# A graph layer on one core: the result is brought to token order by VectorE in 32x32 blocks, with channels laid out to match

## Chip, cores, metric

The kernel runs on one core of a Trainium2 chip. The metric is the device time of one execution in microseconds, as the median of several runs. The first runs of the kernel before gave 1919.82 us (1917.07 to 1921.12, three runs). All ratios below are taken between runs on the same chip in the same call.

## The reference

Input x has 32 batches of 512 tokens with 256 channels; adj has 32 matrices of 512x512, symmetric, with zeros and ones. All is float32. Cut to what matters (`_bn`, `_conv1d` and the set-up of weights are left out):

```python
h0 = relu(layernorm(x))                                   # h below; "x" of the inner layer
xc = transpose(h0)                                        # channels x tokens
h = relu(_bn(_conv1d(xc, conv1_w, 0)))                    # 1 tap
h = _bn(_conv1d(h, conv2_w, 8))                           # 17 taps
x_conv = transpose(relu(h + xc))
s = h0 @ w_se.T + b_se                                    # 3 features
A = exp(-dist(s, s)) * adj
msg = relu(h0 @ w_msg.T + b_msg)
x_nmp = einsum('bnm,bmd->bnd', A, msg)
gi = concat([x_conv, x_nmp]) @ w_ih.T + b_ih              # 768 columns: r, z, n
gh = h0 @ w_hh.T + b_hh
r, z = sigmoid(gi_r + gh_r), sigmoid(gi_z + gh_z)
n = tanh(gi_n + r * gh_n)
return x + (1 - z) * n + z * h0
```

## The kernel before

The program has five stages. The 32 batches come in two halves of 16. Each half has a *conv stage* (normalise, transpose to channels, conv1, a Fourier transform along the tokens; in the first half also that of the weights) and then a *node loop* (messages, A, aggregation, with the Fourier products between them). At the end a *gate stage* works through 16 pairs of batches with the gate products, the blend, and the result. The conv and gate stages are emitted in a fixed order; the node loops are ordered by a scheduler. Inside the gate stage everything lies as channels x tokens, so the result has to be turned to tokens x channels before x can be added and the sum stored.

The parts that the change touches (cuts marked with `# ...`):

```python
work  = ... tc.tile_pool(name="work",  bufs=2)      # lasts over both halves
early = ... tc.tile_pool(name="early", bufs=1)
# pools "first" (conv stage) and "nodes" (node loop) open and close in turn, in the same room

def load_x(b, queue=nc.sync):
    X[b] = pools["work"].tile([P, NC, D], FP, tag="x", name=f"x_{b}", bufs=3)
    queue.dma_start(X[b], x[b].rearrange("(p c) d -> p c d", c=NC))

def normalise(b):
    mv, rstd = STATS.pop(b)
    XN[b] = X[b]                                    # in place
    # ...

def transpose_h(b):
    # ... hT and hs: two tiles of channels x tokens from one PSUM bank
    for dc in range(DC):
        # ... four TensorE transposes into p
        nc.vector.tensor_scalar(HT[b][:, dc, :], p, 0.0, None, op0=ALU.max)
        nc.scalar.activation(HS[b][:, dc, :]..., p.rearrange("p (c q) -> p q c", c=NC), AF.Relu)
    nc.sync.dma_start(HD[b], HT[b])

def message(b):                                     # node loop
    # ...
    nc.tensor.matmul(p[:, : D + NS], HT[b][:, ic, c * P : (c + 1) * P], wmsg[:, ic, :], ...)

def affinity(b):                                    # node loop
    # ...
    nc.vector.transpose(at..., ADJ[b].rearrange("p j (q c) -> p c j q", c=NC)[:, mc])
    nc.vector.tensor_mul(..., by_chunk(at))         # both read with a step of four floats

def finish(p, j, chunks=((0, 1), (2, 3)), wait_for=None):   # gate stage
    xb = XP[p][j]
    # ...
    for bk, i, c, dc in sorted(todo, ...):          # 8 per batch, 256 in all
        nc.tensor.transpose(bk[:, i, dc * P : (dc + 1) * P], NT[p][:, dc, j, c * P : (c + 1) * P], ident)
    for bk, cs in zip(banks, chunks):
        nc.vector.tensor_add(xo, xo, bk[:, : len(cs)])
        nc.sync.dma_start(out[b]..., xo)

def first_part(g, xf, between):                     # conv stage of half g
    for b in range(b0, b0 + 3):
        if b not in X:
            load_x(b)
    statistics(b0)
    normalise(b0)
    statistics(b0 + 1)
    if g == 0:
        transpose_h(b0)
    normalise(b0 + 1)
    if g > 0:
        transpose_h(b0)
    # ...
```

Of the kernel before, what the change touches and what calls it, by code (L numbers as in the profile page):

```python
# [57 lines left out]
def gnn_layer(  # L58
# [40 lines left out]
    X, ADJ, XN, HT, HS, H1, MSG, A, NMP, ST, SL, SR = ({} for _ in range(12))  # L99
    XP, HP, NP, CP, YT, RZ, NT = ({} for _ in range(7))  # L100

    def load_x(b, queue=nc.sync):
        X[b] = pools["work"].tile([P, NC, D], FP, tag="x", name=f"x_{b}", bufs=3)
        queue.dma_start(X[b], x[b].rearrange("(p c) d -> p c d", c=NC))


    load_x(0)
# [10 lines left out]
    nc.scalar.dma_start(w1, w1T.rearrange("(c p) o -> p c o", p=P))  # L118
# [7 lines left out]
    at, n = {}, 0  # L126
    for name in VEC:
        w = GC if name in ("b_ih", "b_hh") else DC
        at[name] = vec[:, n : n + w]
        n += w  # L130
    brz = consts.tile([P, 2 * DC], FP, name="brz")
    nc.vector.tensor_add(brz, at["b_ih"][:, : 2 * DC], at["b_hh"][:, : 2 * DC])
    b_in, b_hn = at["b_ih"][:, 2 * DC :], at["b_hh"][:, 2 * DC :]

    def batch_norm(k):
        scale = consts.tile([P, DC], FP, name=f"{k}_scale")
        shift = consts.tile([P, DC], FP, name=f"{k}_shift")
        nc.vector.tensor_scalar(scale, at[k + "_v"], BN_EPS, None, op0=ALU.add)
        nc.gpsimd.tensor_tensor(scale, scale, minus_half[:, :DC], op=ALU.pow)
        nc.vector.tensor_mul(scale, scale, at[k + "_g"])  # L140
        nc.vector.tensor_mul(shift, at[k + "_m"], scale)
        nc.vector.tensor_sub(shift, at[k + "_b"], shift)
        return scale, shift

    scale1, shift1 = batch_norm("bn1")
    scale2, shift2 = batch_norm("bn2")

# [12 lines left out]
    for c in range(DC):  # L160
# [8 lines left out]
        partial(nc.sync.dma_start, wmsg[:, :, :D], w_msgT.rearrange("(c p) o -> p c o", p=P)),  # L169
        partial(nc.sync.dma_start, wmsg[:, :, D:], w_seT.rearrange("(c p) t -> p c t", p=P)),  # L170
        partial(nc.sync.dma_start, bmsg[:, :D], b_msg.to_broadcast([P, D])),
        partial(nc.sync.dma_start, bmsg[:, D:], b_se.rearrange("t o -> o t").to_broadcast([P, NS])),
    ]
# [55 lines left out]

    def statistics(b):  # L230
# [11 lines left out]
    def normalise(b):  # L242
        mv, rstd = STATS.pop(b)
        XN[b] = X[b]
        for c in range(NC):
            nc.vector.tensor_scalar(
                XN[b][:, c, :], X[b][:, c, :], mv[:, c, 0:1], rstd[:, c : c + 1],
# [4 lines left out]


    def by_chunk(t):

        return t.rearrange("p (q c) -> p c q", c=NC)

    def transpose_h(b):
        HT[b] = work.tile([P, DC, N], FP, tag="hT", name=f"hT_{b}")
        HS[b] = pools["first"].tile([P, DC, N], FP, tag="hs", name=f"hs_{b}", bufs=2)  # L260
        for dc in range(DC):
            p = bank(f"phT_{b}_{dc}")
            for c in range(NC):
                nc.tensor.transpose(p[:, c * P : (c + 1) * P], XN[b][:, c, dc * P : (dc + 1) * P], ident)  # L264
            nc.vector.tensor_scalar(HT[b][:, dc, :], p, 0.0, None, op0=ALU.max)
            nc.scalar.activation(HS[b][:, dc, :].rearrange("p (q c) -> p q c", c=NC),  # L266
                                 p.rearrange("p (c q) -> p q c", c=NC), AF.Relu)
        nc.sync.dma_start(HD[b], HT[b])
        if b % GB != GB - 1:
            del HT[b]  # L270
        del XN[b]

    def conv1(b):
        H1[b] = pools["first"].tile([P, NC, D], FP, tag="h1", name=f"h1_{b}", bufs=2)
        h = N // D
        for c0 in range(0, NC, h):
            p = bank(f"pc1_{b}_{c0}").rearrange("p (c d) -> p c d", d=D)
            for j in range(h):
                c = c0 + j
                for ic in range(DC):  # L280
                    nc.tensor.matmul(p[:, j, :], HS[b][:, ic, c * P : (c + 1) * P], w1[:, ic, :],  # L281
# [4 lines left out]
        del HS[b]  # L286
# [26 lines left out]
    def product(pw, g, u, xf):  # L313
# [21 lines left out]
        nc.scalar.copy(y[:, 0:2, :], p.rearrange("p (k d) -> p k d", d=D))  # L335
        if u == 0:
            nc.vector.memset(y[:, 2, :], 0.0)
        else:
            nc.vector.tensor_copy(y[:, 2, :], p2[:, :D])
# [12 lines left out]

    def message(b):
        MSG[b] = pools["nodes"].tile([P, NC, D], FP, tag="msg", name=f"msg_{b}", bufs=3)
        ST[b] = pools["nodes"].tile([P, 2, NC, NS], FP, tag="st", name=f"st_{b}", bufs=2)
        h = N // D
        for c0 in range(0, NC, h):
            m = MSG[b][:, c0 : c0 + h, :]
            for j in range(h):
                c = c0 + j  # L360
                p = bank(f"pm_{b}_{c}")
                for ic in range(DC):
                    nc.tensor.matmul(p[:, : D + NS], HT[b][:, ic, c * P : (c + 1) * P], wmsg[:, ic, :],  # L363
# [16 lines left out]
    def factors(b):  # L380
# [9 lines left out]
        nc.scalar.copy(t, p)  # L390

    def affinity(b):
# [7 lines left out]
        for mc in range(NC):  # L400
# [3 lines left out]
            nc.vector.transpose(at.rearrange("p (j k) -> p j k", k=32), ADJ[b].rearrange("p j (q c) -> p c j q", c=NC)[:, mc])  # L404
            nc.vector.tensor_mul(*(t.rearrange("p (c q) -> p c q", c=NC) for t in (A[b][:, mc, :], e)), by_chunk(at))  # L405
# [26 lines left out]
    def combine_weights():  # L432

        steps = []
        for k, src in enumerate((w_hhT, w_ihT[D:], w_ihT[:D])):
            w, t = (pools["sums"].tile([P, n, 3, P], FP, tag=f"w{n}", name=f"w{n}_{k}") for n in (4, 7))
            a = src.rearrange("(c p) (g i o) -> p c i g o", p=P, i=2, o=P)
            for j in range(4):
                nc.sync.dma_start(w[:, j], a[:, j // 2, j % 2])
            a11, a21, a12, a22 = (w[:, j] for j in range(4))  # L440
            for dst, x1, x2, op in ((Q5, a21, a22, ALU.add), (Q6, t[:, Q5], a11, ALU.subtract),
                                    (Q7, a11, a21, ALU.subtract), (Q3, a12, t[:, Q6], ALU.subtract)):
                steps.append(partial(nc.gpsimd.tensor_tensor, t[:, dst], x1, x2, op=op))
            stores = [(Q1, a11), (Q2, a12), (Q4, a22)] + [(q, t[:, q]) for q in (Q5, Q6, Q7, Q3)]
            steps[-1] = partial(self_and_store, steps[-1], k, stores)
        return steps

    def self_and_store(step, k, stores):
        step()
        for q, src in stores:  # L450
            nc.sync.dma_start(WS[k][:, q], src)
# [22 lines left out]
    def load_pair_x(p):  # L474
        XP[p] = []
        for b in (2 * p, 2 * p + 1):
            load_x(b)
            XP[p].append(X.pop(b))
# [12 lines left out]
    def inverse(p):  # L491

        CP[p] = pools["ops"].tile([P, 7, N], FP, tag="cp", name=f"cp_{p}")
        for j in range(2):
            for oc in range(DC):
# [7 lines left out]
                xq, hq = (t.rearrange("p (c q) -> p c q", c=NC) for t in (xc, HP[p][:, 2 * oc + j, :]))  # L503
# [355 lines left out]
```

## Time and profile before

| | kernel before |
|---|---|
| median of the first three runs | 1919.82 us |
| span of the profiled run | 1919.7 us, clock 0.991 |
| TensorE busy | 1880.5 us, 98% |
| VectorE, ScalarE, GpSimd busy | 61%, 29%, 29% |
| the result's TensorE transposes | 256 |

The span is the time from the first to the last instruction of the profiled run. The clock is the TensorE clock that was granted, as a share of full speed. An engine is busy while it has an instruction in work, and it is off the path where no other engine waits for it. To evacuate is to copy a result out of the PSUM bank that TensorE wrote it to.

The profile is read from the engine that has no slack. TensorE is that engine here, so the useful question for every instruction is whether TensorE performs it or waits for it. The prediction shows the page, the stages and the groups that carry this; they aren't repeated. One view of the kernel before is added because the argument later turns on it. It is the timeline of the loads of x for the second half and of that half's first transposes (columns: start in us, duration, engine, line, operation, output<-inputs, count).

```profile
135.15 1.10 SPq L104 DMA_DIRECT2D x<-in_x_dram  x1
...
478.98 1.04 PE L264 MATMUL phT<-ident,x 128*128 128x128 f32 x8
481.11 3.78 PE L281 MATMUL pc<-w,hs 128*128 128x256 f32 x16 [1.09 <-ACT hs L266]
```

The second half's first x was asked for before the *first* half's conv stage had ended, more than 300 us ahead of its use; the next load followed at 145 us, and both batches were normalised by 159 us. No bracket with a wait follows the line at 478.98: TensorE goes from the last Fourier product of the node loop straight on to the transposes of the second half.

### The profile page before, as it was taken

Reading aid. Unit: us, or ns where it says so; the run is one execution under the profiler, and the core shown is the slowest. Engines: PE = TensorE matmul, PEld = TensorE weight load, DVE = VectorE, ACT = ScalarE, POOL = GpSimd, SP = SyncE. Lnnn points to the kernel's source line nnn. Section 1 sums busy time; section 2 is a strip of 40 time slices with the busy share of each in tenths; the row PEclk is TensorE's granted clock in tenths of the full one; section 3 lists DMA queues with packets and bytes.
Section 4 is the critical chain, followed back from the end, with each engine's and each line's share of the span. In section 5 each row is a group of like instructions: output and inputs, shape, how many; then the busy total and the mean of one; then the engine's idle time right before and its main releaser. Section 6 shows DMA issues by size and latency. Waiting matters only on the chain.

```text
span 1919.7 us, 21244 instructions
## 1 busy us (share of the span) xinstructions
PE 1880.5 (98%) x7232; PEld 1142.9 (60%) x7232; DVE 1166.6 (61%) x2197; ACT 556.8 (29%) x994; POOL 562.7 (29%) x554
## 2 busy tenths in 40 slices
PE   7999999999999999999999999999999999999998
PEld 5776666666887666765545555555545554555453
DVE  6876777675886667676255535553555445544565
ACT  3665323332444232232212222122212221222121
POOL 3231443433332344445321232213221322133210
PEclk8999999999999999999999999999999999999999
DMA  7998888875668887878342144304440344124400
GB/s 202 297 283 242 248 234 241 258 205 174 204 208 213 236 268 226 254 223 275 93 129 74 55 129 129 100 37 122 129 124 29 106 129 129 37 92 129 129 31 36
DMA packets 220474, 309.87 MB, mean 161 GB/s; under 512 B 14807, under 2 KB 158711, under 8 KB 220367
## 3 DMA queue, kind: packets, MB, share of 16 engines
q1 hardware_dynamic: 200895, 250.93, 44.6%
q0 software_dynamic: 7248, 25.73, 5.0%
q10 hardware_dynamic: 12224, 31.86, 4.6%
q8 instruction: 58, 0.95, 0.2%
q14 instruction: 49, 0.40, 0.1%
HBM read 201.57 MB, written 106.89 MB: 161 GB/s over the span
## 4 chain that ended last, share of the span: by engine, by line
PE 94%; DVE 3%; DMA 2%; issue 0%; ACT 0%; SPq 0%; POOL 0%; DVEq 0%; ACTq 0%; POOLq 0%
PE pg L511 29%; PE pn L511 15%; PE pn L413 11%; PE py L334 11%; PE pc L500 6%; PE pc L281 6%; PE pm L363 5%; PE px L295 3%; PE pw L214 2%; PE pd L399 2%; PE phT L264 1%; PE po L635 1%; PE psr L388 1%; DMA wd<-wst 1%; DMA wt<-wd 0%
## 5 line engine op out<-in xcount | busy, mean ns | idle before, releaser
L511 PE MATMUL pg<-hp,sw 128*128 128x512 f32 x448 | 229.7, 595 | 1.7 <-DVE u L543 1.7
L511 PE MATMUL pg<-np,sw 128*128 128x512 f32 x448 | 229.8, 595 | 0.0
L511 PE MATMUL pg<-cp,sw 128*128 128x512 f32 x448 | 229.1, 593 | 0.0
L413 PE MATMUL pn<-A,msg 128*128 128x512 f32 x512 | 225.0, 593 | 0.0
L489 POOL TENSOR_TENSOR hp<-hp 128x512 f32<-128x512 f32 x64 | 83.1, 1309 | 464.1 <-DMA hp<-hd 331.4
L413 PEld LDWEIGHTS pn<-A,msg 128*128 128x128 f32 x512 | 97.3, 190 | 110.4 <-issue 107.7
L327 POOL TENSOR_TENSOR both<-xf 128x256 f32<-128x256 f32 x78 | 72.8, 934 | 302.4 <-PE py L334 277.4
L405 DVE TENSOR_TENSOR A<-e,at 128x512 f32<-128x512 f32 x128 | 149.0, 1205 | 18.3 <-ACT e L402 18.2
L526 ACT ACTIVATE rz<-rz,brz 128x512 f32<-128x512 f32 x96 | 69.3, 721 | 301.6 <-DVE rz L530 301.6
L334 PE MATMUL py<-wt,both 128*128 128x256 f32 x624 | 151.9, 387 | 3.5 <-DMA adj<-in_adj_dram 3.5
L511 PEld LDWEIGHTS pg<-cp,sw 128*128 128x128 f32 x448 | 85.6, 191 | 107.5 <-issue 107.5
L511 PEld LDWEIGHTS pg<-np,sw 128*128 128x128 f32 x448 | 85.6, 191 | 107.4 <-issue 107.4
L489 POOL TENSOR_TENSOR cp<-cp 128x512 f32<-128x512 f32 x64 | 80.3, 1265 | 221.2 <-ACT cp L505 220.0
L334 PEld LDWEIGHTS py<-wt,both 128*128 128x128 f32 x624 | 115.5, 192 | 47.6 <-issue 31.4
L511 PEld LDWEIGHTS pg<-hp,sw 128*128 128x128 f32 x448 | 82.8, 190 | 94.1 <-issue 88.9
L404 DVE STREAM_TRANSPOSE at<-adj 128x512 f32<-128x512 f32 x128 | 134.6, 1091 | 0.0
L281 PE MATMUL pc<-w,hs 128*128 128x256 f32 x512 | 123.3, 397 | 3.0 <-ACT hs L266 3.0
L500 PEld LDWEIGHTS pc<-back,yt 120*128 120x128 f32 x1024 | 116.9, 192 | 7.6 <-issue 7.6
L311 POOL TENSOR_TENSOR wsum<-wt 128x512 f32<-128x512 f32 x78 | 101.7, 1303 | 67.0 <-DMA wt<-wd 60.0
L363 PE MATMUL pm<-wmsg,hT 128*128 128x259 f32 x512 | 118.1, 383 | 0.0
L500 PE MATMUL pc<-back,yt 120*128 120x80 f32 (+1 forms) x1024 | 116.2, 274 | 0.0
L511 PE MATMUL pn<-hp,sw 128*128 128x512 f32 x224 | 115.2, 596 | 0.0
(113 smaller groups left out, 2821.7 us busy)
## 6 DMA issues: line engine op xcount, KB each, us to landing
wt<-wd SPq DMA_DIRECT2D x160, 256.0 KB, 4.9
adj<-in_adj_dram SPq DMA_DIRECT2D x128, 256.0 KB, 5.6
yd<-y ACTq DMA_DIRECT2D x80, 384.0 KB, 5.1
yt<-yd SPq DMA_DIRECT2D x60, 480.0 KB, 9.8
wd<-wst SPq DMA_DIRECT2D x64, 320.0 KB, 5.2
x<-in_x_dram SPq DMA_DIRECT2D x38, 512.0 KB, 5.6
hd<-hT SPq DMA_DIRECT2D x32, 512.0 KB, 4.3
nd<-nmp SPq DMA_DIRECT2D x32, 512.0 KB, 3.9
```

The costliest lines, as they stand in the source:

```text
L281: nc.tensor.matmul(p[:, j, :], HS[b][:, ic, c * P : (c + 1) * P], w1[:, ic, :], start=(ic == 0), stop=(ic == DC - 1))
L311: nc.gpsimd.tensor_tensor(t, WT[g, u][:, 0], WT[g, u][:, 1], op=ALU.add)
L327: nc.gpsimd.tensor_tensor(both[:, 0], re, im, op=ALU.add)
L334: nc.tensor.matmul(dst, v[:, ic, :], w[:, ic, :], start=(ic == 0), stop=(ic == DC - 1))
L363: nc.tensor.matmul(p[:, : D + NS], HT[b][:, ic, c * P : (c + 1) * P], wmsg[:, ic, :], start=(ic == 0), stop=(ic == DC - 1))
L404: nc.vector.transpose(at.rearrange("p (j k) -> p j k", k=32), ADJ[b].rearrange("p j (q c) -> p c j q", c=NC)[:, mc])
L405: nc.vector.tensor_mul(*(t.rearrange("p (c q) -> p c q", c=NC) for t in (A[b][:, mc, :], e)), by_chunk(at))
L413: nc.tensor.matmul(p, MSG[b][:, mc, dc * P : (dc + 1) * P], A[b][:, mc, :], start=(mc == 0), stop=(mc == NC - 1))
L489: nc.gpsimd.tensor_tensor(t[:, dst, :], t[:, a, :], t[:, b, :], op=sub)
L500: nc.tensor.matmul(bk[:, t0:t1], YT[p][j * W + w][:, oc * P : (oc + 1) * P], back[:, u0 : u0 + t1 - t0], start=(w == 0), stop=(w == W - 1) ...
L511: nc.tensor.matmul(bk, sw[:, k, q, o, :], terms[k][q], start=(first and i == 0), stop=(i == len(ks) - 1), skip_group_check=True)
L526: nc.scalar.activation(rz[:, g, j, :], src, AF.Sigmoid, bias=brz[:, g : g + 1], scale=1.0)
```

## The change

The intent is to take the 256 transposes of the result off TensorE. The VectorE transposes of both kernels work within 32x32 blocks (the prediction names the page on this). So the channels are put in a new order, in which 32-channel pieces of each quarter alternate between the two halves, and x, the weights and the vectors are loaded to match. A block transpose of the result by VectorE then lies as the output wants it. With the tokens in plain order, adj needs no step of four floats in the node loop; instead ScalarE makes the chunks of the message matmuls by copying h (`hq`). The second copy of the transposed h (`hs`) goes. The core of the diff (loads of the vectors and weights, the combination of the gate weights, and the last pair's code are cut):

```diff
     def load_x(b, queue=nc.sync):
-        X[b] = pools["work"].tile([P, NC, D], FP, tag="x", name=f"x_{b}", bufs=3)
-        queue.dma_start(X[b], x[b].rearrange("(p c) d -> p c d", c=NC))
+        X[b] = pools["first"].tile([P, NC, D], FP, tag="x", name=f"x_{b}", bufs=3)
+        queue.dma_start(X[b], x[b].rearrange("(c p) d -> p c d", p=P))
 ...
     def normalise(b):
         mv, rstd = STATS.pop(b)
-        XN[b] = X[b]
+        XN[b] = pools["first"].tile([P, NC, D], FP, tag="xn", name=f"xn_{b}", bufs=2)
 ...
     def transpose_h(b):
-        HS[b] = pools["first"].tile([P, DC, N], FP, tag="hs", name=f"hs_{b}", bufs=2)
 ...
-            nc.scalar.activation(HS[b][:, dc, :].rearrange("p (q c) -> p q c", c=NC),
-                                 p.rearrange("p (c q) -> p q c", c=NC), AF.Relu)
 ...
     def message(b):
+        hq = pools["nodes"].tile([P, DC, N], FP, tag="hq", name=f"hq_{b}", bufs=2)
+        for ic in range(DC):
+            nc.scalar.copy(chunks(hq[:, ic, :]), by_chunk(HT[b][:, ic, :]))
 ...
-                    nc.tensor.matmul(p[:, : D + NS], HT[b][:, ic, c * P : (c + 1) * P], wmsg[:, ic, :],
+                    nc.tensor.matmul(p[:, : D + NS], hq[:, ic, c * P : (c + 1) * P], wmsg[:, ic, :],
 ...
-            nc.vector.transpose(at.rearrange(...), ADJ[b].rearrange("p j (q c) -> p c j q", c=NC)[:, mc])
-            nc.vector.tensor_mul(*(t.rearrange("p (c q) -> p c q", c=NC) for t in (A[b][:, mc, :], e)), by_chunk(at))
+            nc.vector.transpose(at.rearrange(...), ADJ[b][:, :, 32 * mc : 32 * (mc + 1)])
+            nc.vector.tensor_mul(A[b][:, mc, :], e, at)
 ...
+    def to_tokens(p, j, dc):
+        if (p, j) not in OUT:
+            OUT[p, j] = pools["late"].tile([P, N // 32, D // 4], FP, tag="o", name=f"o_{p}_{j}", bufs=2)
+        nc.vector.transpose(OUT[p, j][:, :, 32 * dc : 32 * (dc + 1)], NT[p][:, dc, j, :].rearrange("p (j k) -> p j k", k=32))
+
+    def finish(p, j):
+        last = p == B // 2 - 1
+        for dc in range(0 if last else DC):
+            to_tokens(p, j, dc)
         xb = XP[p][j]
-        (eight TensorE transposes, two sums from PSUM, two stores)
+        nc.vector.tensor_add(xb, xb, OUT.pop((p, j)))
+        for g in range(4):
+            queue = nc.scalar if last and g % 2 else nc.sync
+            queue.dma_start(quarter(out[2 * p + j], g), xb[32 * g : 32 * (g + 1)])
```

The line in parentheses stands for the loops shown under the kernel before, and `(...)` for unchanged text.

## The prediction

> **What bounds the kernel now.** I read the page first: its busy totals, its slices and its chain of waits.
>
> ```profile
> span 1919.7 us, 21244 instructions
> PE 1880.5 (98%) x7232; PEld 1142.9 (60%) x7232; DVE 1166.6 (61%) x2197; ACT 556.8 (29%) x994; POOL 562.7 (29%) x554
> ...
> PE   7999999999999999999999999999999999999998
> ...
> PE 94%; DVE 3%; DMA 2%; issue 0%; ACT 0%; SPq 0%; POOL 0%; DVEq 0%; ACTq 0%; POOLq 0%
> ```
>
> TensorE is busy from the second slice to the last but one, and 94% of the chain that ended last is TensorE. No other engine passes 61%. So time on VectorE or ScalarE counts only where TensorE waits for it, and a TensorE instruction removed counts in full. To see where TensorE waits I asked for sums over five stretches, which are the kernel's stages: conv and DFT of the first half, its node loop, conv and DFT of the second half, its node loop, and the gate stage (columns: stretch, its length, then busy time and instructions of each engine, clock, DMA share, GB/s).
>
> ```profile
> 0.00:174.00 174.00, 159.15 (x901) 115.00 (x902) 128.79 (x367) 98.59 (x207) 48.19 (x75) 0.97 0.90 260
> 174.00:451.00 277.00, 273.13 (x1101) 184.12 (x1100) 200.46 (x393) 84.33 (x160) 105.44 (x107) 0.99 0.81 233
> 451.00:596.00 145.00, 137.99 (x740) 117.47 (x739) 102.37 (x262) 64.48 (x138) 46.46 (x52) 0.98 0.62 204
> 596.00:901.00 305.00, 299.86 (x1202) 201.15 (x1201) 212.44 (x406) 89.97 (x170) 130.20 (x135) 0.99 0.83 238
> 901.00:1920.00 1019.00, 1010.36 (x3297) 525.15 (x3295) 522.52 (x769) 219.43 (x321) 232.44 (x187) 1.00 0.32 96
> ```
>
> TensorE is idle for 14.9, 3.9, 7.0, 5.1 and 8.6 us in them, 39.5 us together. That is all that a change of waits alone could give back. The largest single piece is the 8.9 us before the first matmul.
>
> **What the Trainium skill says.** Four places bear on it.
> (1) "TensorE: Matmul & The Clock Gate", Part 4: a TensorE transpose goes to PSUM and took about 275 ns in one kernel. The trace agrees on the duration, 273 ns for each of the 256 transposes of the result, but the duration is not the cost, because they overlap. The timeline at the first result shows the cost:
>
> ```profile
> 984.81 1.04 PE L635 MATMUL po<-ident,nt 128*128 128x128 f32 x8
> ...
> 985.68 1.02 PE L511 MATMUL pg<-hp,sw 128*128 128x512 f32 x2
> ...
> 990.83 1.04 PE L635 MATMUL po<-ident,nt 128*128 128x128 f32 x8
> ```
>
> Eight transposes hold the next matmul back from 984.81 to 985.68, 0.87 us, or 109 ns each.
> (2) "VectorE: DVE Perf Modes", The three transpose paths: VectorE transposes only 32x32 blocks, and into SBUF. That is why the diff must give the channels a new order (32-channel pieces of each quarter, alternating between the two halves) in x, the weights, the vectors and h: each 32-channel block then lands where the output wants it. The trace has such a transpose already, on adj.
> (3) "SBUF — State Buffer", Door 1: SBUF lines are 16 bytes, and full rate needs two or more accesses in each line. The kernel before reads adj and the transposed adj with a step of four floats, which is 16 bytes. The trace agrees: the product A takes 1205 ns for 512 elements with that step, while other VectorE products of that shape take 692 ns.
>
> ```profile
> L405 DVE TENSOR_TENSOR A<-e,at 128x512 f32<-128x512 f32 x128 | 149.0, 1205 | 18.3 <-ACT e L402 18.2
> L404 DVE STREAM_TRANSPOSE at<-adj 128x512 f32<-128x512 f32 x128 | 134.6, 1091 | 0.0
> L626 DVE TENSOR_TENSOR nt<-nt,rz 128x512 f32<-128x512 f32 x64 | 44.3, 692 | 2.2
> L638 DVE TENSOR_TENSOR x<-x,po 128x512 f32<-128x512 f32 x64 | 41.0, 682 | 63.5 <-PE po L635 63.5
> L635 PE MATMUL po<-ident,nt 128*128 128x128 f32 x256 | 33.7, 273 | 2.3 <-DVE nt L626 2.3
> L266 ACT ACTIVATE hs<-phT 128x512 f32<-128x512 f32 x64 | 36.8, 597 | 56.5 <-DVE hT L265 56.5
> ```
>
> (4) The same VectorE page, in its section on the TRN2 errata, gives (N+151)/0.96 ns for an fp32 sum of two tensors. For 512 that is 691 ns and the trace has 692, so I use it for 1024 elements: 1224 ns, an estimate.
>
> **The change, part by part.**
> *Gate stage, TensorE.* All 256 transposes go: 32 batches x 0.87 us = 27.8 us. They sit inside a stage where TensorE is dense, so all of it is on the path except the last few, which belong to the tail. This is the main term: **-27.8 us**.
> *Gate stage, VectorE.* 64 sums from PSUM (41.0 us) go. In come 64 block transposes and 32 sums of 1024. The transposes read a step of one here, so I take 0.69 us rather than 1.09 (an estimate: the rate of the 692 ns row). That makes 44 + 39 = 83 us, net +42, so VectorE is busy about 565 of 990 us, 57%. A batch is one block of 2 x 0.69 + 1.22 = 2.6 us, put between two products of 2.6 us (six matmul passes of 0.43 us), and the operations that it delays release banks only a product later. Eight banks, and none now used for the result: **0 us**.
> *Tail.* Here VectorE is the path. Before:
>
> ```profile
> 1911.71 0.68 DVE L530 TENSOR_TENSOR rz<-u,pg 128x512 f32<-128x512 f32 x1
> ...
> 1912.42 0.72 ACT L526 ACTIVATE rz<-rz,brz 128x512 f32<-128x512 f32 x1 [2.08 <-DVE rz L530]
> ...
> 1914.65 0.66 PE L635 MATMUL po<-ident,nt 128*128 128x128 f32 x4 [1.39 <-DVE nt L626]
> ```
>
> From 1911.71 it takes 8.0 us to the end. In the diff, batch 0's last transpose and its whole sum (0.65 + 1.2 us) stand in VectorE's order ahead of that first sum, where before one sum of batch 0 filled the wait for the sigmoid. Then come a transpose (0.69) in place of four TensorE ones (0.66), a sum of 1024 in place of the last half (+0.5), and a store in 256-byte pieces on two queues. +1.9 + 0.5 + some 0.5 for the store, less what no longer queues behind three sums (0.6): **+2.5 us**.
> *Conv stages.* The second evacuation of the transposed h by ScalarE (36.8 us) goes, and conv1 reads VectorE's copy. ScalarE evacuated only after VectorE had (56.5 us of its idle time ended so), so the first conv1 of each half starts some 0.6 us earlier: -1.2. The second batch-norm and the bias sum leave the start, where VectorE and GpSimd do them before the first matmul: -0.7. In the second half, a GpSimd step on the gate weights waits 8.0 us for DMAs that read the same tile, and the statistics behind it hold TensorE up for 2.7 us at 564 us. With ScalarE's copies, one store goes out of the sums tile and the loaded weights are free earlier, so most of that should go: -2. x comes in 1 KB instead of 4 KB pieces, and h normalised gets its own buffers, so x's come free earlier; I count 0. Together: **-4 us**.
> *Node loops.* VectorE loses 128 x (1.205 - 0.69) = 66 us and, if the transposes follow, 128 x 0.4 = 51 us of 413. TensorE is idle only 9.0 us in both loops and not for those operations, so this gives nothing. In comes a new step between the load of h and the messages: two ScalarE copies of some 0.6 us per batch (64 x 0.6 = 38 us). ScalarE is 30% busy there. In the timeline h is loaded at 265.9 and used at 284.4, 18 us later with a landing time of 4.8 us, so the copies fit, apart from the start of each loop: **+1 us**.
> *Other ScalarE work.* y in two copies instead of one (some +14 us over both loops) and nine copies of weights, beside TensorE: 0.
> The sum: 1919.8 - 27.8 + 2.5 - 4 + 1 = 1891.5. As the relieved VectorE and ScalarE may give a little more back, I say **1890 us**, 1.6% less.
>
> **Rivals.**
> *A: the copies of h become a wait.* ScalarE takes its work in order. If the copies stand behind a y copy that waits for products just ahead of the messages, TensorE waits about 0.6 + 2 x 0.6 us, 1.8 us in each of some 30 batches, +54 us: the gain is lost, 1930 to 1945. For it: the copies are written just ahead of the messages. Against it: node loops aren't under the manual schedule, the scheduler may put them where h lands, and ScalarE has 70% idle. Chance 8%; half of it would still end near 1910.
> *B: VectorE in the gate stage holds banks.* A block of 2.6 us (3.4 if the transposes still take 1.09) delays evacuations. A wait of 0.5 us, twice a pair, would be +16 us. The profile is against it: VectorE waits for TensorE in that stage (63.5 us in 14 cases ahead of the result's sums alone), not the reverse.
> *C: the relief counts.* If waits for banks in the conv stages go with the second evacuation, up to a third of the 22 us idle there returns, -7 more: 1883. For it: ScalarE is busy 99 of 174 us there; against: 8.9 us of it is the start.
> *D: small pieces.* x and out move in 256-byte pieces in the gate stage. adj's 256 KB in 512-byte pieces take 5.6 us to land, as x's 512 KB do, so this may halve the rate; at a DMA share of 0.32 and with a pair of 61 us to hide in, it shows only in the tail.
>
> **Range and chances.** The main term is firm to 1 us. Tail and conv stages are each uncertain by 3 to 5, and rivals B and C pull to either side: 1881 to 1901. The 2% line is at 1881.4, where C would have to come in full: 0.13. Over 1958 nothing leads but A at its worst: 0.02.
>
> **What would show it.** After the change: no TensorE transposes in the gate stage and a pair's period of 61.2 us instead of 63.0; the product of A near 0.69 us; block transposes near 0.69 us; ScalarE's copies of h early, with no TensorE wait on them; last TensorE matmul 8 to 11 us before the end. Wrong if the messages wait for ScalarE, if gate matmuls wait for VectorE, or if the conv stages move by over 8 us.

## The result and the profile after

The changed kernel took 1913.93 us (median of four runs, 1912.07 to 1915.55); the kernel before took 1918.59 us in the same rounds (1917.07 to 1921.12). The ratio is 0.9974, with a 95% interval of 0.9957 to 0.9991. A ratio here is the mean time of one kernel's fast runs over that of the other's of the same rounds, so it is not quite the ratio of the medians. The result is correct. The gain is 0.26%, where 1.6% had been predicted, and 1913.93 lies outside the range of 1881 to 1901.

The page of the changed kernel: span, busy totals, and two rows of the slices.

```profile
span 1912.2 us, 20928 instructions
PE 1850.5 (97%) x6976; PEld 1112.5 (58%) x6976; DVE 1128.8 (59%) x2231; ACT 564.6 (30%) x1083; POOL 572.4 (30%) x554
...
PE   7999999999698999999999999999999999999997
...
PEclk9999999999799999999999999999999999999998
```

TensorE lost its 256 instructions and 30 us of busy time, as it should, but the span went down by only 7.5 us. Both rows show a new hole in the eleventh slice (478 to 526 us): TensorE's share falls to 6 and its granted clock to 7. Of the sums over the same five stretches, the third and the last say most.

```profile
451.00:596.00 145.00, 125.18 (x662) 105.47 (x661) 103.90 (x284) 43.71 (x103) 46.51 (x50) 0.93 0.53 184
...
901.00:1912.00 1011.00, 993.66 (x3065) 502.70 (x3063) 570.40 (x806) 219.52 (x321) 259.34 (x200) 0.99 0.42 100
```

In the third stretch TensorE is idle for 19.8 us instead of 7.0, at a clock of 0.93 instead of 0.98. In the last one it is idle for 17.3 us instead of 8.6, and the DMA share rose from 0.32 to 0.42 with the small pieces. TensorE's own waits name the cause of that and of two smaller losses (columns: waiter, releaser, us in total, times, longest us).

```profile
PE phT L287 <- DVE xn L276: 18.9, 4, 10.0
...
PE pm L394 <- ACT hq L386: 6.9, 5, 2.7
PE pc L300 <- DVE hT L288: 4.8, 2, 3.7
PE pg L553 <- DVE u L585: 3.1, 1, 3.1
```

The 8.9 us at the start, left out here, are the same as before. The first transposes of h wait 10.0 us for the normalised x, the messages wait for the copies of h, and one gate product waits 3.1 us for VectorE.

The stretches with fixed borders cut through stages that have moved, so I cut both traces at events instead. All numbers are differences of start times in the timelines: A runs from the start to the first message matmul; B to the start of the last matmul of the first half; C from there to the second half's first transpose (0.2 us where TensorE doesn't stop); D runs to the second half's first message; E to the first inverse transform; F to the start of the last gate matmul; G to the end.

| us | A | B | C | D | E | F | G | span |
|---|---|---|---|---|---|---|---|---|
| before | 174.5 | 304.3 | 0.2 | 117.4 | 304.6 | 1009.6 | 9.1 | 1919.7 |
| after | 175.8 | 300.8 | 10.4 | 121.6 | 302.8 | 986.3 | 14.6 | 1912.2 |
| difference | +1.3 | -3.5 | +10.2 | +4.2 | -1.8 | -23.3 | +5.5 | -7.5 |

The main term is there: the gate stage is 23.3 us shorter. The beginning of the second half (C and D) gives 14.4 us of it back, and the tail 5.5. A and D end at the first message matmul, so they hold 1.7 and 1.0 us of the wait for the copies of h. The timeline at the beginning of the second half shows how (in brackets: idle time before, and what ended it).

```profile
477.51 1.53 SPq L109 DMA_DIRECT2D x<-in_x_dram  x3
483.49 1.41 DVE L264 BATCH_NORM_STATS2 stats<-x 128x6 f32<-128x256 f32 x4 [7.38 <-DMA x<-in_x_dram]
...
486.50 1.38 DVE L276 TENSOR_SCALAR xn<-x,mv,rstd 128x256 f32<-128x256 f32 x4 [1.13 <-POOL rstd L270]
487.06 2.21 PE L287 MATMUL phT<-ident,xn 128*128 128x128 f32 x8 [10.03 <-DVE xn L276]
492.93 5.33 PE L300 MATMUL pc<-w,hT 128*128 128x256 f32 x16 [3.66 <-DVE hT L288]
```

The loads of x leave at 477.5 us, when TensorE's last work of the first half (py, 476.01 to 477.04) is already over. Landing, statistics and normalising then follow one another while TensorE stands still. In the kernel before the same loads had left at 135 and 145 us. Afterwards the sixteen conv1 matmuls take 5.33 us, where the kernel before took 3.78 us for the same group. The Trainium skill, "TensorE: Matmul & The Clock Gate", section "Why this matters for your kernels", warns of TensorE gaps over about 3 us because one idle window puts the clock back to its lower state. The trace agrees: the granted clock is 0.50 from 487 to 493 us, and the conv1 matmuls start 0.43 us apart at first and 0.22 us at the end.

### The profile page after: what moved, and what is told of

It reads as the page before. It is cut to its first block, busy times and chain, and to the rows that moved or that the text cites. A ratio compares the mean times of both kernels' runs of the same rounds, so it can differ in the third digit from the quotient of the medians.

```text
span 1912.2 us, 20928 instructions
## 1 busy us (share of the span) xinstructions
PE 1850.5 (97%) x6976; PEld 1112.5 (58%) x6976; DVE 1128.8 (59%) x2231; ACT 564.6 (30%) x1083; POOL 572.4 (30%) x554
## 4 chain that ended last, share of the span: by engine, by line
PE 83%; DVE 3%; DMA 2%; POOL 1%; ACT 1%; issue 0%; SPq 0%; ACTq 0%; DVEq 0%; POOLq 0%
PE pg L553 29%; PE pn L553 15%; PE pn L444 11%; PE py L354 11%; PE pm L394 6%; PE pc L542 6%; PE pc L300 2%; PE pd L430 2%; PE px L315 1%; DMA sw<-ws 1%; PE psr L419 1%; DMA ws<-w 1%; PE phT L287 1%; DVE stats L264 0%; DMA hT<-hd 0%
## 5 line engine op out<-in xcount | busy, mean ns | idle before, releaser
L531 POOL TENSOR_TENSOR hp<-hp 128x512 f32<-128x512 f32 x64 | 93.9, 1478 | 462.7 <-DMA hp<-hd 395.0
L347 POOL TENSOR_TENSOR both<-xf 128x256 f32<-128x256 f32 x78 | 59.3, 760 | 336.7 <-PE py L354 303.3
L436 DVE TENSOR_TENSOR A<-e,at 128x512 f32<-128x512 f32 x128 | 115.6, 943 | 32.1 <-ACT e L433 32.0
L300 PE MATMUL pc<-w,hT 128*128 128x256 f32 x512 | 123.5, 397 | 4.8 <-DVE hT L288 4.8
L394 PE MATMUL pm<-wmsg,hq 128*128 128x259 f32 x512 | 118.1, 382 | 6.9 <-ACT hq L386 6.9
L331 POOL TENSOR_TENSOR wsum<-wt 128x512 f32<-128x512 f32 x78 | 111.4, 1428 | 40.4 <-DMA wt<-wd 27.8
L542 PEld LDWEIGHTS pc<-back,yt 120*128 120x128 f32 x1024 | 116.9, 192 | 7.7 <-issue 7.7
L630 ACT ACTIVATE nt<-nt,vech 128x512 f32<-128x512 f32 x64 | 46.2, 722 | 233.9 <-DVE nt L629 233.9
```

The costliest lines, as they stand in the source:

```text
L300: nc.tensor.matmul(p[:, j, :], HT[b][:, ic, c * P : (c + 1) * P], w1[:, ic, :], start=(ic == 0), stop=(ic == DC - 1))
L331: nc.gpsimd.tensor_tensor(t, WT[g, u][:, 0], WT[g, u][:, 1], op=ALU.add)
L347: nc.gpsimd.tensor_tensor(both[:, 0], re, im, op=ALU.add)
L394: nc.tensor.matmul(p[:, : D + NS], hq[:, ic, c * P : (c + 1) * P], wmsg[:, ic, :], start=(ic == 0), stop=(ic == DC - 1))
L436: nc.vector.tensor_mul(A[b][:, mc, :], e, at)
L531: nc.gpsimd.tensor_tensor(t[:, dst, :], t[:, a, :], t[:, b, :], op=sub)
```

## Experiments

Eleven kernels ran on the chip; all ratios are against the kernel before in the same call, where its medians were 1918.89, 1918.52 and 1919.06 us. All but the one-look run were timed, and all states compared are fast. The theory was, by size: x for the second half comes late, because its tile moved from the lasting pool "work" into the conv stage's own pool "first"; VectorE is behind at the last pair; the tail is longer than counted; the copies of h hold TensorE. The main rivals were that the transposes had not been worth 27.8 us, and that the copies of h or the smaller pieces of the transfers are what costs.

### 1. The transposes alone

The kernel before, with VectorE adding the untransposed result (a wrong result on purpose: relative error 0.63).

```diff
-        for bk, i, c, dc in sorted(todo, key=lambda t: t[3] == wait_for):
-            nc.tensor.transpose(bk[:, i, dc * P : (dc + 1) * P], NT[p][:, dc, j, c * P : (c + 1) * P], ident)
-            nc.vector.tensor_add(xo, xo, bk[:, : len(cs)])
+            nc.vector.tensor_add(xo, xo, NT[p][:, cs[0] // 2, j, :].rearrange("p (c d) -> p c d", d=D))
```

> The kernel before without its 256 TensorE transposes; VectorE adds untransposed data from SBUF in their place (wrong result on purpose). Theory: each group of eight holds TensorE for 0.87 us in a dense stage, so 32 x 0.87 = 27.8 us go, but where TensorE already waits in the last pair (1.67 us for VectorE's u) a removed group only lengthens the wait: 1918.6 - 26 = about 1892. Rival: the transposes were filler in a stage that other engines bound too, waits take their place, and the time stays above 1908.

Measured: 1892.11 us against 1918.89, ratio 0.9866 (0.9853 to 0.9880). The medians differ by 26.8 us, and F fell by 27.1, from 1009.6 to 982.5. In a steady pair the first inverse matmul of a pair follows that of the pair before after 61.22 us instead of 62.97. The changed kernel's steady pairs take 61.22 us too. The timelines of two such matmul groups, first of the kernel before, then of this run:

```profile
944.18 7.26 PE L500 MATMUL pc<-back,yt 120*128 120x72 f32 x64
...
1007.16 7.26 PE L500 MATMUL pc<-back,yt 120*128 120x72 f32 x64
```

```profile
940.21 7.26 PE L500 MATMUL pc<-back,yt 120*128 120x72 f32 x64
...
1001.44 7.26 PE L500 MATMUL pc<-back,yt 120*128 120x72 f32 x64
```

The 14 steady pairs give 24.5 of the 27.1 us, the last pair 2.6. So the main term was right in size, and the gain was lost elsewhere.

### 2. x back in the lasting pool

Simply putting x back was tried first, and it can't be built. The build stopped with: `Not enough space for pool "nodes" with 65.1875 kb per partition`, with 59.5625 left. The node loop's pool is 5.6 KB too large beside x, and the new hq alone takes 8 KB. So room had to be made: hq in halves with three buffers, and one buffer each for at and sr.

```diff
-        X[b] = pools["first"].tile([P, NC, D], FP, tag="x", name=f"x_{b}", bufs=3)
+        X[b] = pools["work"].tile([P, NC, D], FP, tag="x", name=f"x_{b}", bufs=3)
-        hq = pools["nodes"].tile([P, DC, N], FP, tag="hq", name=f"hq_{b}", bufs=2)
+        hq = [pools["nodes"].tile([P, N], FP, tag="hq", name=f"hq_{b}_{ic}", bufs=3) for ic in range(DC)]
-            ... tag="at", name=f"at_{b}_{mc}", bufs=2)
+            ... tag="at", name=f"at_{b}_{mc}", bufs=1)
-        ... tag="sr", name=f"sr_{b}", bufs=2)
+        ... tag="sr", name=f"sr_{b}", bufs=1)
```

> The changed kernel with x's buffers of the conv stages back in the pool that lives through the node loop; for the room, hq in half tiles with three buffers and at and sr with one buffer. Theory M (memory): x moved into a pool whose room the node loop uses before it, so the loads of the second half can't start until the node loop is over; back in the lasting pool they are issued near 135 to 161 us as before, the wait of 10.2 us ahead of the second half's first transposes falls under 1 us, the four later microseconds at a lower clock go too, and the time is 1913.9 - 14 = 1900 (1897 to 1903). Rival: the wait comes from statistics or normalising into the new xn buffers, and the time stays near 1914.

The control has all of these lines but the first pair, so that it differs from this run in x alone.

> Control for x_in_work: the changed kernel with only the smaller buffers (hq in half tiles with three buffers, at and sr with one). Theory M: no difference from the changed kernel, 1914 within 2 us, the wait of 10 us at 477 us stays. Rival: the fewer buffers hold up the node loop and cost 3 us or more.

Measured: 1902.9 us, ratio 0.9922 (0.9910 to 0.9934), with x in "work". The control took 1918.64 us, 0.9995 (0.9985 to 1.0005), over 14 runs that spread from 1913.0 to 1922.9. The place of x's tile is therefore worth 0.9995 - 0.9922 = 0.0073, 14 us of 1919. Against the changed kernel itself the gain is 11 us. The smaller buffers don't help: the control's median is 4.7 us above the changed kernel's, where no difference was expected, and by the ratios they cost some 0.2%. The timeline with x in "work":

```profile
130.77 0.40 SPq L109 DMA_DIRECT2D x<-in_x_dram  x1
...
480.15 1.48 DVE L276 TENSOR_SCALAR xn<-x,mv,rstd 128x256 f32<-128x256 f32 x4 [1.13 <-POOL rstd L270]
...
482.28 4.21 PE L300 MATMUL pc<-w,hT 128*128 128x256 f32 x9 [4.04 <-DVE hT L288]
```

x is loaded at 131 us again and the gap C is back at 0.2 us, but D stays at 122.7 us, 5.3 more than before. The line at 480.15 shows why: the *second* batch of the half is normalised only now, and VectorE does that ahead of the evacuation (hT) that conv1 waits for. In the kernel before normalising was in place, in the lasting tile, so both batches were normalised by 159 us. The new xn tiles live in "first": the first batch was normalised at 475.4 us, and the second batch's statistics stand behind it in VectorE's order (477.0 us).

### 3. The same with another order

```diff
         statistics(b0)
         normalise(b0)
+        if g > 0:
+            transpose_h(b0)
         statistics(b0 + 1)
         if g == 0:
             transpose_h(b0)
         normalise(b0 + 1)
-        if g > 0:
-            transpose_h(b0)
```

> x_in_work with the second half's first transposes (and the copy of h out of PSUM) written ahead of the statistics and normalising of its second batch. Theory: in x_in_work the second half still starts late because only x's buffers came back, not the new xn: batch 17 is normalised after the node loop instead of before it, and its 4 us stand in VectorE's order ahead of the copy that the first conv1 waits for (3.7 to 4.0 us, then lower clock). With the new order that wait goes: 1902.9 - 4 = 1899. Rival: the work only moves behind, the next transposes wait for it, and the time stays at 1903.

Measured: 1897.31 us, 0.9888 (0.9871 to 0.9905). D is 116.9 us, which is 0.5 less than before. With experiment 2 this accounts for the whole loss in C and D: 10.2 us from x's place and queue, and the rest from the order on VectorE.

### 4. The first loads issued by GpSimd

x stays in "first", but the first loads of a half are issued by GpSimd, and don't stand in SyncE's order behind the store of nd at 475.20 and the loads of the gate weights at 475.57.

```diff
             if b not in X:
-                load_x(b)
+                load_x(b, nc.gpsimd)
```

> The changed kernel with the first three x loads of each half issued by GpSimd instead of SyncE. Theory M says that the room comes free when the last tile of the node loop in that room has been read: if that is near 456 us (the last transposes of adj), GpSimd can issue them after its last sum at 466 us, the wait of 10.2 us shrinks to about 3 us and the time to 1905; then part of the wait is SyncE's order (its loads stand behind the last store of nmp at 475 us and the gate weights). If the loads still go out at 477 us, the room alone decides and the time stays at 1914.

Measured: 1906.32 us, 0.9939 (0.9927 to 0.9950). The loads left at 466.7 to 468.3 us and C fell from 10.4 to 2.9 us. So the room had been free by 466.7, and some 11 us of the delay were SyncE's order of work alone. In this run the first statistics start at 475.86 us, straight behind VectorE's last work of the node loop and without a wait for the load. So what is left of C is VectorE's order and the chain from the statistics to xn, no longer the load. Moving the tile made the late load possible; the queue made it later still.

### 5. VectorE behind at the last pair

The changed kernel's timeline at the start of the last pair:

```profile
1848.64 2.08 PE L553 MATMUL pg<-hp,sw 128*128 128x512 f32 x2 [3.12 <-DVE u L585]
1850.51 1.91 PE L553 MATMUL pg<-np,sw 128*128 128x512 f32 x2
```

and the kernel before at the same place:

```profile
1859.36 0.98 PE L635 MATMUL po<-ident,nt 128*128 128x128 f32 x7 [0.36 <-DVE nt L626]
...
1862.02 1.78 PE L511 MATMUL pg<-hp,sw 128*128 128x512 f32 x2 [1.67 <-DVE u L543]
```

In both, VectorE is still blending the pair before when TensorE wants u (in the changed kernel the last operation of the blends starts at 1847.29, u at 1847.90). The last pair has no inverse transforms ahead of it to give VectorE time. Before, the transposes of the result filled part of this wait; without them it grew from 1.67 to 3.12 us (3.12 in experiment 1 too). Then seven matmuls come some 0.42 us later each than at full rate, 3.0 us in all: the first line and the two after it are 1.87 and 1.70 us apart, where 0.86 is usual. The experiment moves two of the four blends of pair 14 behind the u of pair 15.

```diff
+        def sub_and_blend(i, j):
+            nc.vector.tensor_sub(rz[:, i, j, :], HP[p][:, 2 * i + j, :], nt[:, i, j, :])
+            if not last:
+                blend(p, i, j)
         for i, j in ((0, 0), (1, 1), (1, 0), (0, 1)):
+            if p == B // 2 - 2 and i != j:
+                BLENDS.append(partial(sub_and_blend, i, j))
+            else:
+                sub_and_blend(i, j)
 ...  in gates_rz, behind the two u2 sums:
+        while BLENDS:
+            BLENDS.pop(0)()
+        (the tile RZ of the pair is taken here instead of at the start)
```

> The changed kernel with the last two of the four blends of the last pair but one put behind the sum u2 of the last pair in VectorE's order. Theory: in the last pair TensorE waits 3.1 us for u2 because VectorE still blends, then runs some 4 us at half clock (6 x 0.42 us more); before, eight transposes of the result filled part of that wait. With the new order both go: 1913.9 - 5.6 = 1908.3, first inverse to last gate matmul shorter by 5 to 6 us. Rival: the blends are needed by then (the sigmoids write the same buffer) and the wait moves to the sigmoids: no gain.

Measured: 1909.52 us, 0.9949 (0.9932 to 0.9965). F fell from 986.3 to 982.6 us, less than the 5 to 6 us expected.

```profile
1846.70 1.02 PE L553 MATMUL pg<-hp,sw 128*128 128x512 f32 x2
```

VectorE forms u at 1845.14, and the matmul no longer waits and runs at full rate (1.02 us for two, as elsewhere). Two shorter waits, 1.04 and 0.23 us, came in later in the pair. The interval of the time overlaps a little with that of the changed kernel; the last pair is where the effect is plain. From its first inverse matmul to the last gate matmul it takes 80.6 us, where the changed kernel took 85.2. Part of that is the clock: behind the same wait of 3.12 us this stretch took between 82.2 us (no slow matmul, two runs) and 85.2 us (seven) in nine runs. So 1.6 us of the gain are there in each comparison, and up to 3.0 us more hang on the clock.

### 6. The tail: sums of x in halves

The changed kernel's last microseconds:

```profile
1897.24 1.02 PE L553 MATMUL pg<-cp,sw 128*128 128x512 f32 x2
...
1900.35 1.23 DVE L682 TENSOR_TENSOR xb<-xb,o 128x1024 f32<-128x1024 f32 x1
1901.49 0.68 DVE L572 TENSOR_TENSOR rz<-u,pg 128x512 f32<-128x512 f32 x1
```

The last gate matmul is over at some 1898.3 us, yet its sum (L572) starts at 1901.49, behind a transpose and a whole sum of batch 0. In the kernel before that sum started about 0.5 us after the matmul. Here each x sum is cut into its two halves of 32 columns, and each half is put into the wait for the next sigmoid.

```diff
+                def add_half(j, i):
+                    cols = slice(32 * i, 32 * (i + 1))
+                    xb = XP[p][j][:, :, cols]
+                    nc.vector.tensor_add(xb, xb, OUT[p, j][:, :, cols])
+                    (with the second half of a batch: its four stores)
                 def then(i, j):
+                    while half:
+                        half.pop()()
                     blend(p, i, j)
                     to_tokens(p, j, i)
-                    if i != j:
-                        finish(p, j)
+                    half.append(partial(add_half, j, i))
+                    if (i, j) == (0, 1):
+                        half.pop()()
```

> The changed kernel with the last pair's sum of x in halves of 32 channels per block, each put into VectorE's wait for the next sigmoid. Theory: after the last gate matmul VectorE is the path; batch 0's last transpose and its sum of 1.23 us stand ahead of the last gate sum. In halves the sums fill the waits of 0.8 us, and the last sum has 512 elements: from the last gate matmul to the end 13.1 us instead of 14.6, and 1.5 us off the whole, which the times can hardly show. Rival: strided halves of a sum cost as much as the whole (1.2 us each), and the end comes later.

Measured: G fell from 14.6 to 12.3 us.

```profile
1895.57 0.65 DVE L572 TENSOR_TENSOR rz<-u,pg 128x512 f32<-128x512 f32 x1
1896.15 0.67 DVE L862 TENSOR_TENSOR xb<-xb,o 128x512 f32<-128x512 f32 x1
```

A half sum now starts right behind the sum for the sigmoid, and the last one (at 1899.21) takes 0.69 us instead of 1.23. The timed runs don't show it: 1913.45 us, 0.9972 (0.9961 to 0.9983), with 20 runs from 1907.1 to 1922.2. An effect of 2.3 us is below what that spread lets one see, so it rests on the traces alone: G is 12.0 to 12.3 us in the three runs with half sums, and 14.3 to 14.6 us in the seven that keep the tail of the changed kernel.

### 7. The end's store in larger pieces

The stores of the last pair go out in two transfers of contiguous 2 KB rows per batch instead of four of 256-byte rows (a wrong order of the output on purpose; one look).

```diff
-        for g in range(4):
-            queue = nc.scalar if last and g % 2 else nc.sync
-            queue.dma_start(quarter(out[2 * p + j], g), xb[32 * g : 32 * (g + 1)])
         (the four stores stay for the other pairs)
+        for k in range(2 * last):
+            queue = nc.scalar if k else nc.sync
+            queue.dma_start(out[2 * p + j]...[:, 512 * k : 512 * (k + 1)], xb...[:, 512 * k : 512 * (k + 1)])
```

> The changed kernel whose last pair stores its result in 2 KB pieces, two transfers of 256 KB each, instead of 256-byte pieces, four of 128 KB (lands in the wrong places on purpose). Theory: from the end of VectorE's last sum to the end of the span 3.3 us as before the change instead of 5.4. Rival: the two queues or the wait for the last issue cost it, and it stays above 4.8 us.

Measured: from the end of the last sum to the end of the span it took 3.90 us, where the changed kernel took 5.45 and the kernel before 3.30. So 1.55 of the 2.15 us that the last store had got longer belong to its four transfers of small pieces (the run doesn't part the number of transfers from the size of the pieces). Neither expectation was met exactly. The one time, 1913.42 us, is of unknown state and says nothing more.

### 8. No copies of h

The messages read h directly (wrong on purpose: relative error 0.17).

```diff
-        for ic in range(DC):
-            nc.scalar.copy(chunks(hq[:, ic, :]), by_chunk(HT[b][:, ic, :]))
-                    nc.tensor.matmul(p[:, : D + NS], hq[:, ic, c * P : (c + 1) * P], wmsg[:, ic, :],
+                    nc.tensor.matmul(p[:, : D + NS], HT[b][:, ic, c * P : (c + 1) * P], wmsg[:, ic, :],
```

> The changed kernel without ScalarE's copies of h in the node loop: the messages read h as it lies (wrong result on purpose). Theory: the copies cost TensorE 6.9 us of waits, nearly all at the start of the two loops: the time falls by 5 to 7 us, to 1908. Rival: other waits that these cover (for adj and wt, 3.5 us each in the kernel before) come back and the time falls by less than 2 us.

Measured: 1911.77 us, 0.9962 (0.9948 to 0.9977). That is 2.2 us less than the changed kernel's median, and the intervals overlap. The waits of 6.9 us went, and A and E got 2.4 and 3.0 us shorter. But B got 2.0 us longer (a wait of 2.4 us for wt, as in the kernel before, is back), and C and D 0.9 each. So the rival was nearer, and the copies were not where the gain went.

### 9. All repairs together

x in "work" with the smaller buffers, the order of experiment 3, late blends, half sums, and the copies of h for the first batch of each node loop by VectorE, since ScalarE is late there. It was made to see whether the repairs add up.

```diff
+            copy = nc.vector.tensor_copy if b % GB == GB - 1 else nc.scalar.copy
-            nc.scalar.copy(chunks(hq[:, ic, :]), by_chunk(HT[b][:, ic, :]))
+            copy(chunks(hq[ic]), by_chunk(HT[b][:, ic, :]))
```

> All four mendings at once on the changed kernel: x in the lasting pool (with the smaller buffers), the order of the second half's start, the late blends, the tail in halves, and VectorE in place of ScalarE for the copies of h of the first batch of each node loop. If the causes are separate and add up: 1913.9 - 11 (x, measured) - 4.4 (late blends, measured) - 4 (order) - 2 (tail) - 2 (first copies) = 1890.5, which is the time predicted for the change; first inverse to last gate matmul 980.5 us. Rival: they overlap, or a cause of several microseconds is still missing: 1897 or more.

Measured: 1891.63 us (1890.25 to 1894.69), ratio 0.9859 (0.9844 to 0.9873), with a correct result. It beats both kernels. Its second half starts like this:

```profile
477.88 1.04 PE L287 MATMUL phT<-ident,xn 128*128 128x128 f32 x8
...
479.26 3.88 PE L300 MATMUL pc<-w,hT 128*128 128x256 f32 x16 [0.35 <-DVE hT L288]
```

and TensorE's waits are

```profile
PE phT L287 <- DVE xn L276: 9.3, 3, 3.9
...
PE pm L395 <- ACT hq L387: 2.7, 1, 2.7
...
PE pg L554 <- DVE u L598: 1.1, 1, 1.1
```

The wait of 10.0 us is gone, conv1's sixteen matmuls take 3.88 us again, and the wait in the gate stage is 1.1 us.

The same without the pool's move, with x's first loads by GpSimd and the original buffers:

> The same mendings, but x stays in the conv stages' pool with its first loads issued by GpSimd, and hq, at and sr keep their buffers. Sum: 1913.9 - 7.6 - 4.4 - 3 - 2 - 2 = 1895. If the smaller buffers of all_mended cost the node loop 3 to 5 us, this one is level with it or ahead; if not, all_mended is ahead by 4 us.

Measured: 1896.72 us, 0.9882 (0.9867 to 0.9896). C remains at 2.9 us. The stages of all runs that matter, in the cuts of above:

| us | A | B | C | D | E | F | G | span |
|---|---|---|---|---|---|---|---|---|
| no_transposes | 172.2 | 303.5 | 0.2 | 115.3 | 305.8 | 982.5 | 9.1 | 1888.7 |
| small_buffers | 174.7 | 302.7 | 11.5 | 125.1 | 304.2 | 986.2 | 14.6 | 1919.1 |
| x_in_work | 173.0 | 303.9 | 0.2 | 122.7 | 302.8 | 984.2 | 14.3 | 1901.1 |
| x_in_work_order | 174.2 | 303.5 | 0.2 | 116.9 | 302.8 | 984.2 | 14.4 | 1896.1 |
| x_by_pool | 174.6 | 301.9 | 2.9 | 120.6 | 304.1 | 986.3 | 14.3 | 1904.7 |
| late_blends | 175.8 | 300.8 | 10.9 | 121.5 | 302.8 | 982.6 | 14.4 | 1908.8 |
| tail_halves | 173.8 | 300.8 | 10.2 | 121.6 | 302.8 | 983.8 | 12.3 | 1905.3 |
| no_copies | 173.4 | 302.8 | 11.3 | 122.5 | 299.8 | 985.9 | 14.3 | 1910.0 |
| all_mended | 173.7 | 304.0 | 0.2 | 117.7 | 304.3 | 981.0 | 12.0 | 1892.9 |
| mended_by_pool | 174.2 | 302.0 | 2.9 | 117.5 | 304.2 | 982.8 | 12.1 | 1895.5 |

One look of a kernel varies by some 2 us in a stage that its edit doesn't touch: tail_halves has F at 983.8, where the changed kernel, alike in all pairs but the last, has 986.3; behind the same wait of 3.12 us its last pair met no slow matmul. Differences of that size in one look aren't evidence.

## Why the prediction was wrong

| step of the prediction | predicted | measured |
|---|---|---|
| gate stage, TensorE | -27.8 | F -23.3 (transposes alone: -27.1) |
| tail | +2.5 | G +5.5 |
| conv stages | -4 | A, C, D: +1.3 +10.2 +4.2 = +15.7 |
| node loops | +1 | B, E: -3.5 -1.8 = -5.3 |
| "a little more back" | -1.5 | - |
| sum | -29.8 | -7.5 |

**The failed step is "x comes in 1 KB instead of 4 KB pieces, and h normalised gets its own buffers, so x's come free earlier; I count 0", inside the sum of -4 us.** It looked at the buffers' number and missed their pool. The first changed line of `load_x` puts "first" for "work". A pool that opens and closes with a stage keeps the loads from running ahead over the node loop in between: with x in "first", the earliest load of the second half seen in any run left at 466.7 us. The kernel before relied on that prefetch, and its trace shows it (loads at 135 and 145 us). The runs showed +14.4 us in C and D in the place of 0 (1.0 us of it is the wait for the copies of h at the first message). x's place alone was worth 14 us (experiment 2 against its control; 11 us against the changed kernel), and with the order on VectorE the whole loss went (experiment 3). The room was short because the same change had put hq into the node loop's pool.

The other items of the conv sum were small and mixed. conv1 of the first half did start earlier, at 13.96 us instead of 14.58. The first matmul did not: it waits 8.88 us, before 8.87, so the -0.7 for a shorter start was wrong. The statistics' wait late in the second half went from 2.65 to 1.87 us, not by 2.

**The main term** was right: -27.1 us where the transposes alone were taken away, and 61.22 us for a steady pair, as predicted. "All of it is on the path except the last few" failed at the last pair, where the transposes had filled a wait for VectorE: 3.1 us of wait and, in this run, a slower clock after it. The last pair took 85.2 us, where it had taken 84.8 before with its transposes; experiment 5 brought it to 80.6. A first pair that took 0.7 us longer (43.94 us to the next, before 43.2) is a further part. TensorE waits 0.5 us there for the gate weights (`sw<-ws`). This wait is 0.5 to 2.0 us in all eight runs with x in "first" and absent in the five with x in "work", so it goes with x's place too; how is not shown.

**Rival B** (VectorE in the gate stage holds banks) did not happen in the steady pairs: their period equals that of the kernel that has no transposes on any engine. The estimate of 0.69 us for a block transpose with a step of one held.

```profile
L436 DVE TENSOR_TENSOR A<-e,at 128x512 f32<-128x512 f32 x128 | 115.6, 943 | 32.1 <-ACT e L433 32.0
...
L674 DVE STREAM_TRANSPOSE o<-nt 128x512 f32<-128x512 f32 x64 | 41.8, 689 | 0.1
```

The last number ahead of the second bar is the mean of one in ns: 689 for the transpose. The product A takes 943 on average instead of the 690 foreseen. Its median is 693 ns, but single ones take up to 1762. The kept traces show which: the long ones run beside a tensor instruction of GpSimd. Of the changed kernel's products, 57 had none beside them, and none of these took over 693 ns; all longer ones are among the other 71. The sums of x show the same (18 without, at most 1226 ns; 14 with, up to 2236). The transposes, with one input, show no such effect. No edit tested this. In the changed kernel's timeline, two products together take 1.29 us, and two others 2.36 us when GpSimd works on `wsum`:

```profile
362.81 1.29 DVE L436 TENSOR_TENSOR A<-e,at 128x512 f32<-128x512 f32 x2 [1.26 <-ACT e L433]
...
365.24 2.36 DVE L436 TENSOR_TENSOR A<-e,at 128x512 f32<-128x512 f32 x2
365.34 1.71 POOL L331 TENSOR_TENSOR wsum<-wt 128x512 f32<-128x512 f32 x1
```

So a part of the 1205 ns that the prediction put down to the step was this: the 62 products of the kernel before with no GpSimd tensor instruction beside them have a median of 1085 ns. As the prediction said, this is off the path.

**The tail** was mis-sized. The prediction's own parts add to 2.3 us, not 2.5. VectorE's order costs 2.3 us (experiment 6), and the last store takes 2.15 us longer where 0.5 had been allowed (experiment 7: 1.55 of it from the small pieces and their four transfers). Rival D had placed this cost in the tail, rightly, but the sum carried only 0.5 us of it.

**The copies of h** (rival A) hold TensorE for 6.9 us in five waits, near the starts of the loops, instead of 1; not 54. Of these, 2.8 us lie ahead of the first messages and so fall into A and D. B and E together became shorter by 5.3 us. The waits for transfers in the kernel before (3.5 us for adj, 2.9 for wt) were not there, against 4.1 us of new waits for the copies, so idle time gives 2.2 us. And 19 matmuls behind the two old waits had come at half rate, some 0.2 us later each, where none did behind the new ones. Together this covers the 5.3 us. The prediction foresaw none of it, so it was luck that it made up for a part of the loss. Without the copies hardly anything is gained (experiment 8).

**What stays open:** why the smaller buffers alone are some 0.2% slower than the changed kernel (the spread of 14 runs is wide), and how x's place holds up the gate weights in the first pair.

## What to carry to other kernels

When a diff moves a tile from one pool to another, ask which load or computation the old pool let run ahead, look for it in the trace of before, and count the whole chain (load, statistics, normalise) as exposed if the new pool opens only after the stage that hid it. When work is taken off the bounding engine, look at the first and the last repetition one by one: there the removed work may have been filling a wait. Repair the schedule before judging the idea: here the same idea is worth 0.3% as written and 1.4% with the loads, the order and the tail put right.

## What the Trainium skill lacked or had wrong

- "VectorE: DVE Perf Modes", The three transpose paths, gives one time, for bf16, and no page gives what a step costs a float32 block transpose: 128x512 took 1091 ns with a step of four floats in the source (before) and 685 to 689 ns with a step of one (after).
- "TensorE: Matmul & The Clock Gate", Part 4, gives a transpose's duration but not its cost in a dense stream: 273 ns of duration, 109 ns of cost, and experiment 1 confirmed the cost (1.75 us for the 16 of a steady pair, 109 ns each). The same page's warning of idle gaps held for the changed kernel's profile: behind gaps of 10.0 and 3.12 us the clock fell. But behind the same gap of 3.12 us, nine runs had between none and seven matmuls at half rate.
- The "VectorE: DVE Perf Modes" page's formula for a float32 sum held as a median (1224 ns predicted, 1226 measured for 1024 elements) but not as a mean (1457 ns, up to 2236): it held for the 18 sums with no GpSimd tensor instruction beside them, and not for most of the 14 others.
- No page gives what a final store in 256-byte pieces costs a kernel at its end: 5.45 us from the last sum to the end, against 3.90 us with 2 KB pieces and half as many transfers.
